# A Flamingo block with routed experts: one batch's logits back in its up products, one batch's attention weights by a DRAM trip, three expert loads moved

## Chip, cores and metric

The kernel runs on one core of a Trainium2 chip. The metric is the device time of one execution in microseconds; the kernel before has a median of 514.62 us over 11 runs (514.3 to 515.65). Another kernel's time is read against this.

## The reference, cut to what matters

There are four batches of 512 tokens, 512 wide, and a context of 512 rows, 256 wide, for each batch. All is float32.

```
x = x + tanh(g_xattn) * xattn(layernorm(x), ctx)
x = x + tanh(g_ffn)   * ffn(layernorm(x))

xattn: q = ctx @ Wq.T + bq;  k = ctx @ Wk.T + bk         (128 wide)
       attention = softmax(q @ k.T)                       (512 x 512 for each batch)
       out[l, m] = sum_n logits[l, n] * attention[m, n]   (logits = layernorm(x))

ffn:   shared = (silu(h @ Wg_s) * (h @ Wu_s)) @ Wd_s      (hidden 352)
       probs = sigmoid(h @ Wr + br + rb)                  (8 experts)
       the two highest of the 8, their probabilities over their sum as weights w
       routed = sum over the two of w * (silu(h @ Wg[e]) * (h @ Wu[e])) @ Wd[e]
```

The second sum over n needs the attention weights with n on the partitions: the softmax comes out with m on the partitions and has to be transposed. The same holds for the normalised rows h ahead of the feed-forward part.

## The kernel before, in words

**Memory.** One large tile, `wbig`, holds the eight experts' weights (`EW` columns each), and until they come in the parts behind the first `early = 3` experts are scratch for the attention: context, keys and queries, two transposed weight tiles `attT_v`, two transposed row tiles `xT_v`, the softmax tiles `ex_v`, the normalised tiles `xn_v` and their transposes `xnT_v`. Experts 0 to 2 overlay nothing. `ps_mm` gives four PSUM buffers, taken in turn by projections, energies, gate, up and all small products; `ps_out` two for outputs.

**Order.** Each engine runs its instructions in the fixed order of the built program; a scheduler makes that order from the program's dependencies, and `after(later, earlier)` adds dependencies by hand. SP (SyncE) issues most loads, ACT (ScalarE) those of the hidden tiles, POOL (GpSimd) the stores of tiles to DRAM and all indirect transfers. Each queue is in order too, and an instruction that waits holds up what is behind it. A DMA also waits for the eighth one before it of the same kind, whose semaphore it shares.

**Attention, batch by batch** (loop at lines 623 to 644). `attention_weights(i)` (line 339) projects keys and queries (L344, copied out by ScalarE, L351), makes four energy tiles (L362), and for each the row maximum (L364), the exponential (L367), and the division by the sum (L369, L370). For the first `AT_ONCE = 2` batches TensorE transposes the tiles at once, 128x128 at a time (`transposed`, L300, copied out by VectorE at L303). For later batches POOL stores each tile to DRAM in four column quarters (`to_quarters`, L321), SP loads it back (`from_quarters`, L327) with the rows regrouped, and VectorE turns it in 32x32 blocks (`turn`, L331; `attention_weights_turned`, line 389). This leaves the rows of the transposed tile in another order, which the host's `chunks` gives to the other operand, xT. `attention_out(i - 1)` (line 393) then makes batch i-1's output (L398, four tiles, each of four products that read all four transposed tiles), adds it to x (L402), takes the statistics (L310, L313), the inverse deviation (a power on POOL, L317), normalises (L411), and sends the normalised tiles on the same DRAM trip to `xz_d`. The last batch's normalised tiles are kept and transposed by TensorE (`last_turned`, line 647).

**Shared expert, hidden part.** `shared_hidden` (line 460) makes for each of the four chunks of 128 tokens of a batch four gate products (352 wide) and four up products (L471), SiLU on ScalarE (L479), the product on VectorE (L482), and a store to `hs_d` from ACT's queue. The router's weights stand behind the up weights. Where a batch is not in `alone`, the up products are 360 wide and give the logits (L481); where it is, they are 352 wide, and `logits` (line 443) makes the logits of several chunks by products of their own, 8 wide (L450), which can come ahead of the up products. `amid` lists what is put between the products of a chunk.

**Routing.** `route(b)` (line 498) takes the exponential, the two highest probabilities, and a running count by expert (`pre`, `cum`), each batch on top of the last. `places` (line 523) makes from it by two small products (L527) each token's place in a list, and `scatter_places` (line 557) writes tokens and weights to the list `slot_d` by eight indirect DMAs for each batch (L559). When all are there, POOL loads the list into `tab` (L711); VectorE spreads it (L720), small products (L653) pick each block's part, and from that come the indices by which POOL gathers rows for the routed blocks.

**The rest.** Line 656 on is the part between the attention and the list: batch 2's hidden chunks, batch 3's chunks, counting and expert loads, laid out by hand. Then come 16 tiles of the shared down product (`shared_down`, L575 and L602), with the list's small products behind the fifth and sixth, and 37 routed blocks (L796, L575).

Of the kernel before, what the change touches and what calls it, by code (L numbers as in the profile page):

```python
# [22 lines left out]
def flamingo_block(  # L23
# [17 lines left out]
    B, S, D = x.shape  # L41
# [7 lines left out]
    NS, ND, NCC, NN = S // P, D // P, C // P, N // P  # L49
# [49 lines left out]
    early = 3  # L99
# [104 lines left out]
    def load_expert(e, behind=None, parts=(True, True)):  # L204
        at = e * EW
        for src, f, part in ((wgu, 2 * H, parts[0]), (wd, D, parts[1])):
            n = src.shape[1] // P * f
            if part:
                load = nc.sync.dma_start(
                    out=wbig[:, at : at + n].rearrange("p (c f) -> p c f", f=f),  # L210
                    in_=src[e].rearrange("(c p) f -> p c f", p=P),
                )
                if behind is not None:
                    after(load, behind, "that goes first")
            at += n
# [17 lines left out]
    ones = fconst([P, P], "ones")  # L233
# [99 lines left out]
        )  # L333

    product = {}
    AT_ONCE = 2
    gain = {}

    def attention_weights(b):
# [49 lines left out]
    def attention_weights_turned(b, m, behind):  # L389
        t = turn(ex_v[m].rearrange("p (b w) -> p b w", b=NQ), attT_v[b % 2][:, :, ts(m, P)])  # L390
        after(t, behind, "they come in meanwhile")
# [45 lines left out]
        return turns  # L437

    lg_b = {}
    alone = {B - 2, B - 1}  # L440
    scatters = []

    def logits(b, lo=0, hi=NS):

        if lo == 0:
            lg_b[b] = small.tile([P, NS, E], F32, tag="lg", name=f"lg_{b}")
        pr = ps_mm.tile([P, hi - lo, E], F32, tag="mm", name="pr")
        for s in range(lo, hi):
            for c in range(ND):
                p = nc.tensor.matmul(  # L450
                    pr[:, s - lo, :], lhsT=xnT_v[b % 2][:, c, ts(s, P)], rhs=ws[:, c, 2 * H :],
                    start=(c == 0), stop=(c == ND - 1),
                )
                after(p, product["last"], "not too many small ones at once")
        nc.vector.tensor_tensor(
            lg_b[b][:, lo:hi, :], pr,
            bias_r.rearrange("p (o e) -> p o e", o=1).broadcast_to([P, hi - lo, E]), ALU.add,
        )

    def shared_hidden(b, lo=0, hi=NS, amid={}):  # L460

        route_too = b not in alone
        if route_too and lo == 0:
            lg_b[b] = small.tile([P, NS, E], F32, tag="lg", name=f"lg_{b}")
        wide = HR if route_too else H
        for s in range(lo, hi):
            pg = ps_mm.tile([P, H], F32, tag="mm", name="pg")
            pu = ps_mm.tile([P, wide], F32, tag="mm", name="pu")
            for c in range(ND):
                for dst, at, n in ((pg, 0, H), (pu, H, wide)):  # L470
                    product["last"] = nc.tensor.matmul(  # L471
                        dst, lhsT=xnT_v[b % 2][:, c, ts(s, P)], rhs=ws[:, c, at : at + n],
                        start=(c == 0), stop=(c == ND - 1),
                    )
                if c in amid:
                    amid[c]()
            filled = h_sb[(b * NS + s) % OUT]
            h = filled[:, :H]
            nc.scalar.activation(h, pg, AF.Silu)  # L479
            if route_too:  # L480
                nc.vector.tensor_add(lg_b[b][:, s, :], pu[:, H:], bias_r)  # L481
            done = nc.vector.tensor_mul(h, h, pu[:, :H])  # L482
            at = (b * NS + s) * NQ * P
            to_quarters(filled, hs_d[at : at + NQ * P, :], nc.scalar)
        return done
# [37 lines left out]
    def places(b, at, m1, m2, sel, pre):  # L523

        pl = ps_mm.tile([P, NS * E], F32, tag="mm", name="pl")
        for i, (l, r) in enumerate(((tri, sel), (ones, pre))):
            p = nc.tensor.matmul(  # L527
                pl, lhsT=l, rhs=r.rearrange("p s e -> p (s e)"),
                start=(i == 0), stop=(i == 1),
            )  # L530
            after(p, product["last"], "the routing takes its time")
        place = small.tile([P, NS, E], F32, tag="place", name=f"place_{b}")
        nc.vector.tensor_add(place, pl.rearrange("p (s e) -> p s e", e=E), first)  # L533
        tot = small.tile([P, NS, 1], F32, tag="tot", name=f"tot_{b}")
        nc.vector.tensor_add(tot, m1, m2)
        nc.vector.reciprocal(tot, tot)
        nc.vector.tensor_scalar_mul(tot, tot, tgf)
        todo = []
        for k, m in enumerate((m1, m2)):
            nc.vector.tensor_mul(at[k], at[k], place)  # L540
            pos = small.tile([P, NS, 1], F32, tag=f"pos{k}", name=f"pos{k}_{b}")
            nc.vector.tensor_reduce(pos, at[k], AX.X, ALU.add)
            posi = small.tile([P, NS], I32, tag=f"posi{k}", name=f"posi{k}_{b}")
            nc.vector.tensor_copy(posi, pos.rearrange("p s o -> p (s o)"))
            low = small.tile([P, NS], I32, tag=f"low{k}", name=f"low{k}_{b}")
            nc.vector.tensor_single_scalar(low, posi, P - 1, op=ALU.bitwise_and)
            ent = small.tile([P, NS, 2], F32, tag=f"ent{k}", name=f"ent{k}_{b}")
            nc.vector.tensor_tensor(
                ent[:, :, 0], token[:, b * NS : (b + 1) * NS], low, ALU.subtract
            )  # L550
            nc.vector.tensor_mul(
                ent[:, :, 1], m.rearrange("p s o -> p (s o)"), tot.rearrange("p s o -> p (s o)")
            )
            todo += [(ent[:, s, :], posi[:, s : s + 1]) for s in range(NS)]
        return todo

    def scatter_places(todo, behind=None):
        for what, where in todo:
            sc = nc.gpsimd.indirect_dma_start(  # L559
                out=slot_d, in_=what,  # L560
                out_offset=bass.IndirectOffsetOnAxis(ap=where, axis=0),
                in_offset=None,
            )
            tc.declare_no_dep(sc.ins, group="places", reason="no two tokens share a place")
            tc.add_to_no_dep_group("places", sc.ins)
            after(sc, cleared)
            if behind is not None:
                after(sc, behind, "it delays less there")
            scatters.append(sc)
# [48 lines left out]
    routed = None  # L618
# [4 lines left out]
    for i in range(B):  # L623
        attention_weights(i)
        if i + 2 < B:
            load_context(i + 2)
            load_rows(i + 2)
        if i < early:
            load_expert(i)
        if i > 0:  # L630
            power, done = attention_out(i - 1, halves(i - 2))
            if i + 1 < B:
                load_transposed(i + 1)
            if routed:
                scatter_places(places(i - 3, *routed), power)
        if i >= 2:
            for m in range(NS):
                attention_weights_turned(i, m, done)
                done = shared_hidden(i - 2, m, m + 1)
                if i == B - 1 and m == 0:  # L640
                    load_expert(early, done)
                if i == B - 1 and m == 1:
                    load_expert(early + 1, done, (True, False))
            routed = route(i - 2)
# [6 lines left out]
    def amid(dst, lhsT, rhs):  # L651

        p = nc.tensor.matmul(dst, lhsT=lhsT, rhs=rhs, start=True, stop=True)  # L653
        after(p, product["last"], "not too many small ones at once")

    routed = {}
    load_expert(4, None, (False, True))
    load_expert(5, None, (True, False))
    shared_hidden(B - 2, 0, 1, {1: lambda: logits(B - 2, 0, 2), 3: lambda: logits(B - 2, 2)})
    routed[B - 2] = route(B - 2)  # L660
    step = shared_hidden(
        B - 2, 1, 2, {1: lambda: last_turned(0, 2), 2: lambda: last_turned(2, NS)}
    )
# [1 line left out]
    shared_hidden(  # L665
        B - 2, 2, 3, {
            1: lambda: logits(B - 1, 0, 2), 2: lambda: logits(B - 1, 2),
            3: lambda: scatter_places(places(B - 2, *routed[B - 2])),
        }
    )  # L670
    routed[B - 1] = route(B - 1)
    step = shared_hidden(B - 2, 3)
    load_expert(6, step)
    step = shared_hidden(
        B - 1, 0, 1, {2: lambda: scatter_places(places(B - 1, *routed[B - 1]))}
    )
    back_early(step)

# [1 line left out]
    cum_b = fconst([P, E, JB], "cum_b")  # L680
# [2 lines left out]
    )  # L683
    pn = ps_mm.tile([P, 1], F32, tag="mm", name="pn")
    shared_hidden(
        B - 1, 1, 2, {1: lambda: amid(pn, cum_b.rearrange("p e j -> p (e j)"), ones[:, 0:1])}
    )
    used = fconst([P, 1], "used")
    nc.vector.tensor_tensor(used, pn, thr, ALU.is_gt)
# [26 lines left out]
    done = shared_out(0, 0, NS, (step, done))  # L716
# [240 lines left out]
```

## Time and profile before

| | |
|---|---|
| median of 11 runs | 514.62 us |
| the profiled execution | 514.6 us |
| its span | 512.6 us |
| granted TensorE clock, mean | 0.992 |
| TensorE's longest wait | 1.2 us, at the start |
| batch 1's output product begins, ends | 42.80, 60.15 us |
| batch 2's hidden chunks | 133.59 to 161.95 us |
| batch 3's hidden chunks | 161.95 to about 182.3 us |
| shared down product | 183.03 to about 222.3 us, two tiles later |
| first routed block begins | 223.30 us |
| last matmul ends | about 501.5 us |

The profile names engines PE (TensorE matmul), PEld (its weight loads), DVE (VectorE), ACT, POOL and SP. A float32 product is two records on PE. In a timeline a row is: start, length, engine, line, operation, written tile and read tiles, number of records, and in brackets the idle time before it and what ended that. The slices of the page cut the span into 40 parts; a digit is a busy share in tenths.

### The profile page before, as it was taken

The numbers are of one execution on the slowest core, as the hardware profiler recorded it, in microseconds if no ns is written. First come the engines' busy times: TensorE is split into PE (matmuls) and PEld (weight loads), VectorE is DVE, ScalarE is ACT, GpSimd is POOL, SyncE is SP. The second block draws the span as 40 slices with busy tenths as digits, with TensorE's granted clock in tenths as the row PEclk, the third lists the DMA queues.
The fourth block names the chain that finished last, engine by engine and source line by source line (L and its number), as shares of the span: only waits on it lengthen the run. The fifth ranks groups of instructions, "written<-read, shape, count | busy, mean of one in ns | idle before, by whom it ended". The sixth has DMA issues, their size and how long they took to land. (4 is left out here: it accounts for less than half of the span.)

```text
span 512.6 us, 5473 instructions
## 1 busy us (share of the span) xinstructions
PE 494.8 (97%) x1523; PEld 276.7 (54%) x1523; DVE 230.6 (45%) x542; ACT 93.8 (18%) x167; POOL 264.8 (52%) x293
## 2 busy tenths in 40 slices
PE   8999999999999999999999999999999999999981
PEld 4444464465677645445555555555555555555540
DVE  1898965855855256554223322332332233323210
ACT  3354034111241100000111111111111111111110
POOL 3005220271264702345777777777477777777231
PEclk9999999999999999999999999999999999999996
DMA  6999993579936999624566656665545666556333
GB/s 216 395 371 354 345 352 122 155 176 169 358 101 88 223 205 313 216 83 132 120 139 119 124 123 139 119 125 122 110 118 128 138 123 128 128 132 131 53 41 42
DMA packets 66589, 86.82 MB, mean 169 GB/s; under 512 B 32928, under 2 KB 39968, under 8 KB 66560
## 3 DMA queue, kind: packets, MB, share of 16 engines
q1 hardware_dynamic: 42480, 54.03, 34.8%
q0 software_dynamic: 13184, 25.88, 25.8%
q10 hardware_dynamic: 10896, 6.56, 5.1%
q8 instruction: 15, 0.25, 0.2%
q14 instruction: 14, 0.11, 0.1%
HBM read 55.73 MB, written 30.70 MB: 169 GB/s over the span
## 5 line engine op out<-in xcount | busy, mean ns | idle before, releaser
L761 POOL DMA_INDIRECT x_all<-xz_d,idx x148 | 141.3, 955 | 81.7 <-issue 34.4
L331 DVE STREAM_TRANSPOSE x_all<-x_all 128x512 f32<-128x512 f32 (+1 forms) x71 | 70.0, 986 | 157.1 <-DMA x_all<-by 135.5
L796 PE MATMUL rg<-wbig,x_all 128*128 x296 | 111.9, 460 | 1.7 <-issue 0.9
L796 PE MATMUL ru<-wbig,x_all 128*128 x296 | 111.7, 459 | 0.0
L575 PE MATMUL po<-wbig,x_all 128*128 x222 | 101.4, 592 | 0.7 <-DVE x_all L847 0.7
L796 PEld LDWEIGHTS rg<-wbig,x_all 128*128 128x128 f32 x296 | 55.9, 190 | 43.1 <-issue 18.4
L824 POOL DMA_INDIRECT out_x<-ws,idx x37 | 59.6, 1611 | 31.1 <-ACT ws L823 13.6
L796 PEld LDWEIGHTS ru<-wbig,x_all 128*128 128x128 f32 x296 | 56.2, 190 | 31.3
L575 PEld LDWEIGHTS po<-wbig,x_all 128*128 128x128 f32 x222 | 42.1, 190 | 44.0 <-issue 36.4
L398 PE MATMUL po<-wbig 128*128 128x512 f32 x128 | 56.4, 592 | 0.0
L471 PE MATMUL pg<-ws,wbig 128*128 128x352 f32 x128 | 49.3, 467 | 0.0
L471 PE MATMUL pu<-ws,wbig 128*128 128x360 f32 (+1 forms) x128 | 48.7, 462 | 0.0
L804 ACT ACTIVATE h_all<-rg 128x352 f32<-128x352 f32 x37 | 17.1, 463 | 171.6 <-PE rg L796 171.6
L317 POOL TENSOR_TENSOR rstd<-ve,mhalf 128x4 f32<-128x4 f32 x8 | 8.2, 1022 | 71.3 <-DVE ve L315 37.9
L823 ACT ACTIVATE ws<-po,wts 128x512 f32<-128x512 f32 x37 | 25.4, 687 | 104.2 <-PE po L575 101.2
L575 PE MATMUL po<-wsd,wqk 128*128 128x512 f32 x96 | 42.3, 595 | 0.5 <-DVE eoff_i L706 0.5
L398 PEld LDWEIGHTS po<-wbig 128*128 128x128 f32 x128 | 24.2, 190 | 29.4 <-issue 27.7
L559 POOL DMA_INDIRECT slot_d<-ent,posi x32 | 31.0, 968 | 17.3 <-issue 8.6
L471 PEld LDWEIGHTS pu<-ws,wbig 128*128 128x128 f32 x128 | 24.3, 190 | 13.6 <-DVE place L533 0.2
L575 PEld LDWEIGHTS po<-wsd,wqk 128*128 128x128 f32 x96 | 18.0, 190 | 22.1 <-issue 20.2
L471 PEld LDWEIGHTS pg<-ws,wbig 128*128 128x128 f32 x128 | 23.3, 190 | 11.6 <-issue 0.5
L806 DVE TENSOR_TENSOR x_all<-h_all,ru 128x352 f32<-128x352 f32 x34 | 17.6, 516 | 13.6 <-PE ru L796 7.4
(136 smaller groups left out, 339.2 us busy)
## 6 DMA issues: line engine op xcount, KB each, us to landing
wbig<-in_Wgu SPq DMA_DIRECT2D x8, 1408.0 KB, 12.0
by<-x_all SPq DMA_DIRECT2D x34, 192.0 KB, 3.2
x_all<-by SPq DMA_DIRECT2D x34, 192.0 KB, 2.4
wbig<-in_Wd SPq DMA_DIRECT2D x8, 768.0 KB, 11.0
x_all<-in_x SPq DMA_DIRECT2D x4, 1024.0 KB, 10.5
wbig<-in_xT SPq DMA_DIRECT2D x4, 1024.0 KB, 9.2
xz_d<-wbig POOLq DMA_DIRECT2D x16, 256.0 KB, 4.6
out_x<-x_all SPq DMA_DIRECT2D x16, 256.0 KB, 3.0
```

What stands on the lines that cost most here:

```text
L317: power = nc.gpsimd.tensor_tensor(rstd, ve, mhalf, ALU.pow)
L331: return nc.vector.transpose(dst.rearrange("p c (j b) -> p b c j", b=NQ), z.rearrange("p b (c i) -> p b c i", i=Q))
L398: product["last"] = nc.tensor.matmul(po, lhsT=xT_v[b % 2][:, c, ts(s, P)], rhs=attT_v[b % 2][:, c, :], start=(c == 0), stop=(c == NN - 1),)
L471: product["last"] = nc.tensor.matmul(dst, lhsT=xnT_v[b % 2][:, c, ts(s, P)], rhs=ws[:, c, at : at + n], start=(c == 0), stop=(c == ND - 1),)
L559: sc = nc.gpsimd.indirect_dma_start(out=slot_d, in_=what, out_offset=bass.IndirectOffsetOnAxis(ap=where, axis=0), in_offset=None,)
L575: product["last"] = nc.tensor.matmul(po, lhsT=hT[:, j, :], rhs=wdj(j), start=(j == 0), stop=(j == NF - 1))
L761: g = nc.gpsimd.indirect_dma_start(out=z[:, q, :], out_offset=None, in_=xz_d, in_offset=at(idx4[:, q, i : i + 1]),)
L796: nc.tensor.matmul(dst, lhsT=xgT[:, c, :], rhs=wbig[:, bass.ds(base[i] + (c * 2 * H + lo), H)], start=(c == 0), stop=(c == ND - 1),)
L804: silu = nc.scalar.activation(sg, pg, AF.Silu)
L806: nc.vector.tensor_mul(h[:, :H], sg, pu)
L823: nc.scalar.activation(y, po, AF.Copy, scale=wts[:, i : i + 1])
L824: nc.gpsimd.indirect_dma_start(out=out, in_=y, out_offset=at(idx[:, i : i + 1]), in_offset=None, compute_op=ALU.add)
```

## The change

Three edits, with what they bring along.

- `AT_ONCE` goes from 2 to 1: batch 1's softmax tiles make the DRAM trip and are turned by VectorE, behind `done`, the last normalised tile of batch 0; the host reorders xT for batches 1 to 3 rather than 2 and 3.
- Batch 2 leaves `alone`: its logits come from 360-wide up products. Its routing and batch 3's both come after batch 2's last chunk; their scatters move into batch 3's first and second chunk, and the counting product from behind the second to behind the third step of that chunk.
- Experts 0, 1 and 2 are loaded in the third turn of the loop, each behind a hidden chunk of batch 0, rather than one in each of the first three turns.

```
-    AT_ONCE = 2
+    AT_ONCE = 1
...
-    alone = {B - 2, B - 1}
+    alone = {B - 1}
...
-        if i < early:
-            load_expert(i)
...
+        if i == 1:
+            for m in range(NN):
+                attention_weights_turned(i, m, done)
         if i >= 2:
             for m in range(NS):
                 attention_weights_turned(i, m, done)
                 done = shared_hidden(i - 2, m, m + 1)
+                if i == 2 and m < early:
+                    load_expert(m, done)
...
-    shared_hidden(B - 2, 0, 1, {1: lambda: logits(B - 2, 0, 2), 3: lambda: logits(B - 2, 2)})
-    routed[B - 2] = route(B - 2)
+    shared_hidden(B - 2, 0, 1)
...
     shared_hidden(
         B - 2, 2, 3, {
             1: lambda: logits(B - 1, 0, 2), 2: lambda: logits(B - 1, 2),
-            3: lambda: scatter_places(places(B - 2, *routed[B - 2])),
         }
     )
-    routed[B - 1] = route(B - 1)
     step = shared_hidden(B - 2, 3)
+    routed = {b: route(b) for b in (B - 2, B - 1)}
     load_expert(6, step)
     step = shared_hidden(
-        B - 1, 0, 1, {2: lambda: scatter_places(places(B - 1, *routed[B - 1]))}
+        B - 1, 0, 1, {2: lambda: scatter_places(places(B - 2, *routed[B - 2]))}
     )
...
     shared_hidden(
-        B - 1, 1, 2, {1: lambda: amid(pn, cum_b.rearrange("p e j -> p (e j)"), ones[:, 0:1])}
+        B - 1, 1, 2, {
+            0: lambda: scatter_places(places(B - 1, *routed[B - 1])),
+            2: lambda: amid(pn, cum_b.rearrange("p e j -> p (e j)"), ones[:, 0:1]),
+        }
     )
...
-        "xT": np.concatenate([xT[:2], chunks(xT[2:])]),
+        "xT": np.concatenate([xT[:1], chunks(xT[1:])]),
```

## The prediction

> **What bounds the kernel now.** I read the engine shares and slices of the page first, then TensorE's waits, then each engine's timeline around the three edits, then the single transfers of the routing list.
>
> ```profile
> PE 494.8 (97%) x1523; PEld 276.7 (54%) x1523; DVE 230.6 (45%) x542; ACT 93.8 (18%) x167; POOL 264.8 (52%) x293
> ...
> PE   8999999999999999999999999999999999999981
> ...
> DMA  6999993579936999624566656665545666556333
> ```
>
> TensorE is busy in every slice up to the tail. Each of its waits is 1.2 us or less, so every matmul removed is time gained, and every new wait on TensorE is time lost in full. It runs its instructions in the order of the built program, so the question at each edit is when TensorE arrives at an instruction and when the data does.
>
> The span is 512.6 us, the profiled execution 514.6 us (2.0 around the span), the median of the runs 514.62. I add changes to 514.6. About 0.2% (1 us) is what a measurement of this kernel can tell from no change.
>
> **Part A: second batch's weights by the DRAM trip.** TensorE's timeline (start, length, line, tile):
>
> ```profile
> 22.83 3.60 PE L398 MATMUL po<-wbig 128*128 128x512 f32 x8
> 26.41 0.63 PE L300 MATMUL pt<-ident,wbig 128*128 128x128 f32 x4
> ...
> 34.21 7.03 PE L398 MATMUL po<-wbig 128*128 128x512 f32 x16
> 41.08 1.88 PE L344 MATMUL pp<-wbig,wqk 128*128 128x512 f32 x4
> ...
> 60.15 0.76 PE L471 MATMUL pg<-ws,wbig 128*128 128x352 f32 x2
> ```
>
> One 512-wide product is two records: 34.21 to 41.08 is eight products, 0.859 each. From 22.83 to 60.15 there are 40 of them (16 for batch 0's output, 4 projections and 4 energies of batch 2, 16 for batch 1's output), 34.4 us. The other 2.95 us are batch 1's 16 PE transposes and a 0.43 us wait among them. They go.
>
> What comes in: four stores by POOL, four loads by SP, four VectorE turns. In the built order the turns stand behind all four normalised tiles of batch 0 (the dependency on `done`) and one BN_STATS on batch 3's rows. VectorE's rows of before give the rates:
>
> ```profile
> 41.28 0.75 DVE L402 SCALAR_TENSOR_TENSOR x_all<-po,gain,x_all 128x512 f32<-128x512 f32 x1 [0.67 <-PE po L398]
> ...
> 44.30 2.00 DVE L411 TENSOR_SCALAR wbig<-x_all,mv,rstd 128x512 f32<-128x512 f32 x4 [1.12 <-POOL rstd L317]
> ...
> 55.60 2.02 DVE L331 STREAM_TRANSPOSE wbig<-wbig 128x512 f32<-128x512 f32 x2
> ```
>
> Without the transposes, batch 0's last output product ends near 37.65 (22.83, 16 products and one projection, 0.2 us for a PSUM buffer). Its sum on VectorE starts behind earlier work at 38.55; with its statistics it is at 39.9. The built order then has batch 2's gain ahead of batch 0's variance, so two POOL powers of 1.0 us run one after the other: 42.7. Normalising takes 1.95 (44.65), the BN_STATS 0.6, the four turns 0.95 each: 49.1. All four must be there, since each product reads all four tiles. TensorE would be free at 45.4 (the energies wait until 41.9 for ScalarE, whose key/query copy stands behind an activation that needs batch 2's offset). So batch 1's output runs from 49.2 to 62.95 instead of ending at 60.15: **+2.8 us**. If the two powers overlapped as before (4.7 us from the end of the product to the end of the normalising), it would be +0.5. Behind this wait on TensorE stand all of batch 1's output and the hidden chunks after it; VectorE's sums wait for them. The trip itself is off this path: the last store is issued near 31.4, and batch 2's and 3's stores and loads of the same kind landed in 2.7 to 8.3 us, so I expect its end at 38, at worst near 48, which would cost under 1 us. Batch 3's rows, queued on SP behind the trip's loads, are expected near 43, before the 44.65 at which they are wanted; late by 1 us costs 1 us.
>
> **Part B: third batch's logits in the up products.** Two groups of eight 8-wide products go:
>
> ```profile
> 136.03 1.85 PE L450 MATMUL pr<-ws,wbig 128*128 128x8 f32 x16
> 137.74 0.84 PE L471 MATMUL pg<-ws,wbig 128*128 128x352 f32 x2
> ```
>
> A group costs 1.71 plus 0.07 for the weight load behind it, 1.78. The 16 up products become 360 wide; 16 gate/up pairs took 19.15 us wide (60.15 to 79.30), 18.98 narrow. Net **-3.4**. The last batch's 16 transposes now come 3.5 us sooner after the start of this stage, and their copies stand behind a ScalarE table load and SiLU: about **+0.4**, from nothing to 0.8.
>
> **Part C: the routing of batches 2 and 3 moves behind batch 2's last chunk.** Let T be the end of that chunk on TensorE: 161.95 before; after, 161.95 + 2.8 - 3.4 + 0.4 - 0.44 (a pair of small products moves behind T) = 161.3. For batch 0, with the same scheme, T was 79.30 and the first routing instruction behind the exponential came at 82.12, T+2.8. The two routings now alternate on VectorE; the built order has 30 instructions from there to batch 2's selection, at 0.11 each (0.26 for the reciprocals): T+6.4. TensorE reaches the product with it after one chunk, T+4.75: **a new wait of 1.8** (1.2 to 2.3). Batch 3's other gate/up products stand behind it, and SiLU and VectorE's products wait for those. Then come a gate/up pair and the second product, T+8.2; place to first scatter took 1.6 (157.33 to 158.95): the scatters start at T+10.2, 171.5. Before, they started at T-3.0:
>
> ```profile
> 158.95 0.96 POOL L559 DMA_INDIRECT slot_d<-ent,posi  x1 [7.26 <-DVE ent L548]
> ...
> 178.48 0.96 POOL L559 DMA_INDIRECT slot_d<-ent,posi  x1 [0.30 <-DMA slot_d<-ent,posi]
> 190.26 0.59 POOL L711 DMA_DIRECT2D ws<-slot_d  x1 [10.82 <-DMA hs_d<-h_all]
> ```
>
> The 16 scatters took 19.5 us from first to last issue. The transfers issued at 178.48 and 190.26, with the time to landing last:
>
> ```profile
> slot_d<-ent,posi POOLq DMA_INDIRECT x1, 11.0
> ```
>
> ```profile
> ws<-slot_d POOLq DMA_DIRECT2D x1, 128.0 KB, 4.4
> ```
>
> The list's load left only when the last scatter had landed. TensorE needs the list at a fixed place, the small products behind five tiles of the shared down product:
>
> ```profile
> 183.03 13.14 PE L575 MATMUL po<-wsd,wqk 128*128 128x512 f32 x30 [0.53 <-DVE eoff_i L706]
> 196.01 0.98 PE L653 MATMUL pq<-pick,ws 128*128 128x39 f32 x8
> ```
>
> ```profile
> 195.01 0.74 DVE L720 COPY ws<-ws 128x128 f32<-128x128 f32 x4
> ```
>
> The copies that spread the list ended at 195.75: cover left before, 0.3 us. After: TensorE arrives at 196.0 + 2.8 - 3.4 + 0.4 + 1.8 = 197.6. Last scatter 171.5 + 19.4 = 190.9. Landing: 5.3 at best, 11.0 under the load of the last ones; expert 7's load and the hidden tiles' reads still run then, so nearer the second, 9.5, and 0.8 to the load: 201.2. The list's load 4.0 (4.4 before, 2.7 the least of such a size or double): 205.2. Spread and hand-over 1.3: 206.5. **+8.9**, with ends 3.3 (5.3 and 2.7) and 11. Behind the wait stand the rest of the shared products and the routed blocks; POOL's gathers wait for the same list. They start 5 us behind the small products and take 10; TensorE has 26 us of shared products behind them, so the first routed block does not wait again. Nothing later gives this time back: from 230 to 470 us TensorE is idle for 0.8 us of 240.
>
> The Trainium skill, "DMA: Bandwidth & Descriptors", section "Anatomy of one DMA — SWDGE (gpsimd) path", prices such a transfer at about 2.0 us plus its bytes at 436 GB/s. By it the last scatter would cost 2.0 and the list's load 2.3, the list would be ready at 197.3, and the wait would be gone: 516 in all. The 11.0 and 4.4 us above speak against using it here.
>
> **Part D: the clock.** No wait over 1.2 us stands inside the kernel, so what a long one does is seen only at its ends:
>
> ```profile
> 503.00:504.00 1.00, 0.00 (x0) 0.00 (x0) 0.00 (x0) 0.00 (x0) 0.78 (x1) 1.00 0.00 0
> ...
> 505.00:506.00 1.00, 0.00 (x0) 0.00 (x0) 0.00 (x0) 0.00 (x0) 0.00 (x0) 0.50 0.84 63
> ```
>
> ```profile
> 1.19 3.78 PE L150 MATMUL idle<-h_all 128*128 128x256 f32 x8 [1.19 <-DVE h_all L146]
> ```
>
> The column before the DMA share is the granted clock: it falls to 0.50 some 3.3 us after the last matmul (501.5). And the first eight 256-wide records take 0.45 each, against 0.43 for 512-wide ones later: half speed, for some 4 us. So a wait of 9 us should be followed by about 4 us at half speed: **+2.0** (0 to 2.3). Part A's gap of 3.8 us is on the edge; I count nothing, and keep 2.0 for the upper end.
>
> **Edits at no cost.** Experts 0 to 2 are first read at 223 us and, issued behind chunks near 70 to 82, land by 100 at 400 GB/s; were they late, block 0 would wait, but 120 us cover it. The loads that they stood in front of gain nothing, since TensorE did not wait for them. Batch 1's next reads of normalised rows stand around expert 0's load on SP; they are needed 20 us later. The host's reordering of one more batch of xT moves no work on the chip.
>
> **Sum.** 2.8 - 3.4 + 0.4 + 1.8 + 8.9 + 2.0 = +12.5: 514.6 + 12.5 = **527.1**.
>
> **Rivals.** (1) Short list: with the hidden tiles' reads held back while TensorE stands, scatters land in 5.3 to 7 and the list in 2.7; the wait is 3 to 5 and the clock may not fall: 518 to 522. For it: scatters landed in 5.9 to 7.8 at 160 to 163 us, when the DMA share was 0.20. Against: expert 7 is then loading. (2) Both gaps cost the clock and the landing is the old 11: 529 to 532. (3) Not slower: the list is in time. Place: the small products at 196; price: 10.9 us fall away; it decides if the list's copies are ready by 197.6, 8.9 us sooner than worked out, with Part A at its low end of 0.5: 513.9. Against it: POOL's pace alone puts the last scatter at 190.9, and two transfers follow. (4) The change does nothing to order: excluded by the built program, where the turns, the selection and the scatters stand as said.
>
> **Chances.** Forecast (523 to 529) 0.59; (1) 0.20; (2) 0.15; (3) 0.06, half of it within 0.2%, half faster. Range 518 to 531: it reaches into (1) and (2) and covers 3.3 to 11 for the list. Faster 0.03, same 0.03, slower 0.94.
>
> **What would show it.** Right: TensorE idle some 4 us before batch 1's output, released by VectorE's turns; idle 1.8 before the product with batch 2's selection; idle 7 to 11 before the small products at about 198, and a granted clock under 1 right behind. Scatters from about 171 to 191, their pace unchanged. No product of 8 columns for batch 2. Wrong if the scatters start earlier than T+8, if the last one lands within 6 us, or if TensorE's order has more shared products ahead of the list.

## The result, and the profile after

The changed kernel took **526.31 us** (median of 16 runs, 524.5 to 531.47); the kernel before, run beside it, 515.2 us (62 runs, 513.58 to 518.87). The ratio is 1.0215, with a 95% interval of 1.0198 to 1.0231: slower, by about 2% (11.1 us, where 12.5 was forecast). The first profiled execution took 530.42 us (span 528.6), near the top of its runs. The same kernel was profiled again in run e9: 527.07 us, span 525.3. Both profiles are used below.

The engine shares, slices and clock of the first profile:

```profile
PE 498.5 (94%) x1475; PEld 274.9 (52%) x1475; DVE 230.0 (44%) x544; ACT 91.2 (17%) x165; POOL 268.7 (51%) x297
...
PE   8995999999999893999999999999999999999992
...
PEclk9998899999999998799999999999999999999998
DMA  6989659949976668452465566665645666665532
```

TensorE has 48 records fewer (32 of the logits, 16 transposes), and two dents where it had none: in the fourth slice (near 45 us) and in the sixteenth (near 205 us). At both the clock is down as well. TensorE's chain of waits names them (total, times, longest):

```profile
PE pq L656 <- DVE ws L724: 8.7, 1, 8.7
PE po L398 <- DVE wbig L331: 3.5, 1, 3.5
PE pe L362 <- ACT wbig L351: 2.8, 2, 2.3
PE pl L527 <- DVE at L495: 1.6, 1, 1.6
```

They are the list, the turns of the second batch's weights, ScalarE's key/query copy ahead of the third batch's energies, and the third batch's selection. The first dent, in TensorE's timeline:

```profile
37.93 2.74 PE L344 MATMUL pp<-wbig,wqk 128*128 128x512 f32 x6
...
42.98 5.40 PE L362 MATMUL pe<-wbig 128*128 128x512 f32 x8 [2.32 <-ACT wbig L351]
51.91 14.43 PE L398 MATMUL po<-wbig 128*128 128x512 f32 x26 [3.53 <-DVE wbig L331]
```

and in VectorE's:

```profile
42.60 1.99 DVE L411 TENSOR_SCALAR wbig<-x_all,mv,rstd 128x512 f32<-128x512 f32 x4 [0.99 <-POOL rstd L317]
47.49 0.69 DVE L310 BATCH_NORM_STATS2 st<-x_all 128x6 f32<-128x512 f32 x1 [2.90 <-DMA x_all<-in_x]
48.10 3.76 DVE L331 STREAM_TRANSPOSE wbig<-wbig 128x512 f32<-128x512 f32 x4
```

The normalising ends at 44.6, as worked out. Then VectorE stands 2.90 us for the fourth batch's rows, with the turns behind it. The third batch's energies took 5.40 us for 3.70 before, most of them at half speed. The second dent, in the timelines of TensorE, POOL and VectorE:

```profile
173.70 0.38 PE L527 MATMUL pl<-sel,tri 128*128 128x32 f32 x2 [1.60 <-DVE at L495]
...
189.88 13.04 PE L575 MATMUL po<-wsd,wqk 128*128 128x512 f32 x30
211.65 1.93 PE L656 MATMUL pq<-pick,ws 128*128 128x39 f32 x8 [8.73 <-DVE ws L724]
```

```profile
177.14 0.96 POOL L559 DMA_INDIRECT slot_d<-ent,posi  x1 [16.83 <-DVE ent L551]
...
196.10 0.96 POOL L559 DMA_INDIRECT slot_d<-ent,posi  x1 [0.31 <-issue]
204.13 0.59 POOL L715 DMA_DIRECT2D ws<-slot_d  x1 [7.07 <-DMA h_all<-hs_d]
```

```profile
211.32 0.82 DVE L724 COPY ws<-ws 128x128 f32<-128x128 f32 x4 [7.06 <-DMA ws<-slot_d]
```

The scatters' train lasts 19.0 us from first to last issue, as before (19.5), 18 us later. The last scatter took 7.4 us to land, the list's load leaves 8.0 us behind its issue and takes 7.1 to land; TensorE stands in front of it. In the wait and behind it, the clock column (ahead of the DMA share) in stretches of 2 us:

```profile
208.00:210.00 2.00, 0.00 (x0) 0.00 (x0) 0.00 (x0) 0.00 (x0) 0.00 (x0) 0.54 1.06 407
...
214.00:216.00 2.00, 2.00 (x3) 0.67 (x2) 1.84 (x7) 0.00 (x0) 0.00 (x0) 0.50 0.53 178
```

Half speed lasts from 208.2 to 218.4. The whole difference can be laid out by landmarks of TensorE, each stretch in us:

| stretch | before | predicted | first profile | second profile (e9) |
|---|---|---|---|---|
| start to the third batch's hidden chunks (133.59 before) | 133.59 | +2.8 | +8.6 | +5.0 |
| those chunks (to 161.95) | 28.36 | -3.4 | -3.4 | -2.9 |
| to the shared down product (183.03) | 21.08 | +2.2 | +1.6 | +1.6 |
| to the list's products (196.01) | 12.98 | +8.9 | +8.8 | +9.5 |
| to the down product behind them (199.86) | 3.85 | +2.0 | +3.4 | +2.2 |
| to the first routed block (223.30) | 23.44 | 0 | 0 | 0 |
| to the end of the span | 289.3 | 0 | -3.0 | -2.7 |
| sum | 512.6 | +12.5 | +16.0 | +12.7 |

The pair of small products that moves behind the third batch's last chunk (0.44 us) is taken off in the second row and added in the third. There +1.6 came for +2.2 because a wait of 0.5 us ahead of the shared down product, which the kernel before has, is gone.

### The profile page after: what moved, and what is told of

Same layout as the page of the kernel before. It is cut to its first block, busy times and chain, and to the rows that moved or that the text cites. A ratio compares the mean times of both kernels' runs of the same rounds, so it can differ in the third digit from the quotient of the medians.

```text
span 528.6 us, 5399 instructions
## 1 busy us (share of the span) xinstructions
PE 498.5 (94%) x1475; PEld 274.9 (52%) x1475; DVE 230.0 (44%) x544; ACT 91.2 (17%) x165; POOL 268.7 (51%) x297
## 5 line engine op out<-in xcount | busy, mean ns | idle before, releaser
L398 PE MATMUL po<-wbig 128*128 128x512 f32 x128 | 59.1, 619 | 3.6 <-DVE wbig L331 3.5
L471 PE MATMUL pg<-ws,wbig 128*128 128x352 f32 x128 | 49.2, 466 | 0.0
L575 PE MATMUL po<-wsd,wqk 128*128 128x512 f32 x96 | 44.7, 622 | 0.0
L321 POOL DMA_DIRECT2D bya<-wbig x12 | 9.6, 798 | 37.7 <-DVE pre L520 20.2
## 6 DMA issues: line engine op xcount, KB each, us to landing
wbig<-in_Wd SPq DMA_DIRECT2D x8, 768.0 KB, 10.3
```

The costliest lines, as they stand in the source:

```text
L321: engine.dma_start(out=by.rearrange("(a p) w -> p a w", p=P), in_=src.rearrange("p (a w) -> p a w", a=NQ))
L398: product["last"] = nc.tensor.matmul(po, lhsT=xT_v[b % 2][:, c, ts(s, P)], rhs=attT_v[b % 2][:, c, :], start=(c == 0), stop=(c == NN - 1),)
L471: product["last"] = nc.tensor.matmul(dst, lhsT=xnT_v[b % 2][:, c, ts(s, P)], rhs=ws[:, c, at : at + n], start=(c == 0), stop=(c == ND - 1),)
L575: product["last"] = nc.tensor.matmul(po, lhsT=hT[:, j, :], rhs=wdj(j), start=(j == 0), stop=(j == NF - 1))
```

## The experiments

The twelve runs were made on three chips: e1 to e4 on one, e5 to e8 on a second, e9 to e12 on a third. Each ratio is to the kernel before on the same chip, which took 522.19, 521.67 and 518.78 us there, spread over 7 to 12 us. Why it is above 515 there is what e5 and e11 are about. Effects are therefore read from waits and landmarks first.

**e1: without the trip.** The second batch's weights are turned by TensorE again.

```
-    AT_ONCE = 1
+    AT_ONCE = 2
...
-        if i == 1:
-            for m in range(NN):
-                attention_weights_turned(i, m, done)
...
```

> The changed kernel with the second batch's weights transposed by TensorE again (edit A undone; the later routing and the later expert loads stay). Theory: the list's wait of some 9 us and the slow clock behind it stay, since they come from the later routing; what goes is TensorE's wait for the turns and the clock it costs. 522 to 525 us. Rival 1 (the trip is the whole loss): 511 to 513. Rival 2 (the trip is hidden and costs nothing): 526 to 527. On the trace: no wait of po on a stream transpose near 50 us, a wait of pq of 7 to 11 us near 200.

Measured: 527.06 us, ratio 1.0136 (1.0058 to 1.0215). No wait for turns is left, and the selection still waits 1.6. The list:

```profile
PE pq L653 <- DVE ws L721: 10.8, 1, 10.8
PE pl L527 <- DVE at L495: 1.6, 1, 1.6
```

The time is not the theory's 522 to 525 but the second rival's, and that of the changed kernel on the third chip (e9, 527.49), though the fourth batch's energies start at 85.03 instead of 89.42. Against e9's profile, the first routed block begins only 1.65 us sooner (237.01 for 238.66): the list wait is 1.4 longer and half speed lasts 13.65 us instead of 10.24. The end is 3.6 longer (290.2 from the first block to the span's end, for 286.6). So between these two profiles the trip's cost is real at its place, and is given back at two others.

**e2: without the logits' move.** The third batch's logits, routing and scatters stand as before; trip and experts as in the changed kernel.

```
-    alone = {B - 1}
+    alone = {B - 2, B - 1}
...
-    shared_hidden(B - 2, 0, 1)
+    shared_hidden(B - 2, 0, 1, {1: lambda: logits(B - 2, 0, 2), 3: lambda: logits(B - 2, 2)})
+    routed[B - 2] = route(B - 2)
...
+            3: lambda: scatter_places(places(B - 2, *routed[B - 2])),
...
```

> The changed kernel with the third batch's logits and the whole routing order as before (edit B undone; trip and later expert loads stay). Theory: no wait for the list and none for the selection; left is the trip's price, 1 to 5 us over before: 516 to 520 us. Rival 1 (the trip is the whole loss): 526. Rival 2 (trip free, loss all routing): 512 to 515. On the trace: pq waits under 1 us, po waits 3 to 7 us for the turns.

Measured: 526.13 us, ratio 1.0115 (1.0032 to 1.0198). The list wait is gone. That fits the late dispatch as its cause, but does not show it: the list had landed at 200.8, and TensorE came for it only at 212.97, some 11 us late by other waits and the clock behind them. (e10 shows it.) The longest of these I had not thought of:

```profile
PE pw L656 <- ACT h_all L479: 5.7, 1, 5.7
...
PE pb L656 <- ACT h_all L479: 2.0, 1, 2.0
```

TensorE waits for SiLU to free its gate tile, in the last two hidden chunks. ACT is late because of a store of hidden units (who waited, for what):

```profile
ACT h_all L479 <- DMA hs_d<-wbig: 10.6, 1, 10.6
```

And ahead of that store VectorE had stood for a scatter; e5 takes this step apart.

```profile
DVE ent L551 <- DMA slot_d<-ent,posi: 4.2, 1, 4.2
```

**e3: the list's products four tiles later.**

```
     done = shared_out(0, 0, NS, (step, done))
+    done = shared_out(1, 0, 4)
...
-    shared_out(1, 0, 1)
+    done = shared_out(2, 0, 1)
...
-    shared_out(1, 1, 2)
+    done = shared_out(2, 1, 2)
...
-    shared_out(1, 2)
-    shared_out(B - 2)
+    done = shared_out(2, 2, 4)
```

> The changed kernel with the list's spread and small products put four tiles of the shared down product (10.3 us) later. Theory: the wait of 8.7 us and the slow clock behind it are both gone, some 12 us, and the gathers still end before the first routed block: 513 to 517 us. Rival (the wait only moves, to the first routed blocks, whose rows are gathered 10 us later): 520 to 526, with TensorE idle near 225 to 240 us. On the trace: clock 1.00 from 190 to 240.

Measured: 521.3 us, ratio 1.0019 (0.9977 to 1.0061). No wait for the list is left, but not all of it is won:

```profile
PE po L575 <- DVE wqk L331: 3.6, 1, 3.6
```

TensorE now waits for a hidden tile on its way back from DRAM, whose read landed late beside the last scatters and expert 7's load, and half speed for 3.4 us followed. Of some 12 us (9.5 and 2.2 behind it) 6.6 are gained against e4 beside it (527.91), which has the list at its place.

**e4: experts 0 to 2 loaded early again.**

```
+        if i < early:
+            load_expert(i)
...
-                if i == 2 and m < early:
-                    load_expert(m, done)
```

> The changed kernel with experts 0 to 2 loaded one in each of the first three turns again (third edit undone). Theory: the later loads cost nothing by themselves; undone, their bytes fall into the trip's stretch, stores, loads and the fourth batch's rows land later, and TensorE waits longer before the second batch's output: 527 to 532 us. Rival (the moved loads are what slows the middle of the kernel): 515 to 522. On the trace: the wait for the turns grows from 3.5 us.

Measured: 527.91 us, ratio 1.0152 (1.0069 to 1.0235).

```profile
PE pq L656 <- DVE ws L724: 10.0, 1, 10.0
PE pe L362 <- ACT wbig L351: 3.8, 2, 3.4
...
PE po L398 <- DVE wbig L331: 0.7, 1, 0.7
```

The list wait, and the first routed block at 239.80, lie by those of the changed kernel's two profiles (242.32, 238.66), so the place of these loads is worth nothing that can be told. The theory's longer wait for the turns did not come. It is short, 0.7 us, because the third batch's energies ran later (44.28) and at half speed; the fourth batch's start at 88.49, for 93.05 and 89.42.

**e5: the kernel before, profiled again.** No edit.

> The kernel before, unchanged, profiled a second time. In its first profile POOL issued the list's load at 190.26, it landed 4.4 us later, DVE copied the list from 195.01 and TensorE used it at 196.01: at most about 1 us was to spare. In the runs beside the first four experiments this kernel took 516.3 to 528.0 us, 514 to 519 elsewhere. Theory (the kernel before already stands at the edge of the list wait): where its time is above 515, the chain of TensorE's waits shows a wait for the list's copy of about the excess, at half price again for the clock behind it where the wait is over some 3 us; at 514 to 515 it shows none. Rival (the excess is elsewhere, in the block loop or at the ends): a time above 516 without a row of waiting for the list, and block 0 starting within 1 us of 223.3.

Measured: 525.4 us (span 523.4), beside runs of itself of 517.43 to 526.83. Both theories fell: the list is in time, and the excess is ahead of the routed blocks (233.41 for 223.30), not in them or at the end. TensorE's timeline, and ACT's:

```profile
188.39 0.29 PE L653 MATMUL pw<-pick,eoff 128*1 128x39 f32 x2 [5.35 <-ACT h_all L479]
```

```profile
187.87 0.46 ACT L479 ACTIVATE h_all<-pg 128x352 f32<-128x352 f32 x1 [10.31 <-DMA hs_d<-wbig]
```

It is e2's wait, in the kernel before, and it starts at VectorE. What the scatters write to the list stands in small tiles, two of a kind, taken in turn by the batches. So VectorE can write the fourth batch's entries only when the second batch's last scatter has landed. VectorE's timeline in the first profile, then in e5:

```profile
161.51 0.37 DVE L551 TENSOR_TENSOR ent<-m,tot 128x4 f32<-128x4 f32 x2
```

```profile
161.63 0.17 DVE L551 TENSOR_TENSOR ent<-m,tot 128x4 f32<-128x4 f32 x1
166.40 0.17 DVE L551 TENSOR_TENSOR ent<-m,tot 128x4 f32<-128x4 f32 x1 [4.60 <-DMA slot_d<-ent,posi]
```

That scatter left at 150.73 in the first profile and landed after 10.1 us, less than 1 us before its tile was wanted. In e5 it left at 150.84 and landed after 15.4. Behind VectorE's wait its hidden product began at 167.41 instead of 162.72, and the store of these hidden units left at 167.96 instead of 163.28. Beside the scatters it took 19.4 us instead of 14.0; ACT stood until it had landed, near 187.4, and 5.3 us of TensorE with 6.8 us at half speed followed. Why the second batch's scatter landed later in e5 no run tells.

**e6: the kernel before with the list's products four tiles later** (e3's edit).

> The kernel before with the list's twelve products four output tiles later (behind five tiles of the second batch's and later shared products instead of one), nothing else. Theory (the kernel before stands at the edge of the list wait): the load then has some 12 us to spare, no run of it waits for the list, and the runs draw together near 514 to 516, while the kernel before beside it spreads as far as 528: ratio about 0.985 to 0.995 where the kernel before is spread, 1.00 where it is at 514. Rival (the spread has another cause): the same median and the same spread as the kernel before, ratio 1.00. A price that could show: TensorE waiting 3.6 us for the turn of a hidden tile, as in the changed kernel with the list later.

Measured: 522.0 us (518.82 to 524.67), ratio 1.0006 (0.997 to 1.0042). The rival holds: the same median, the spread hardly less (5.9 us for 9.4), and the wait is that of e5, behind 3.0 us of VectorE for the same scatter:

```profile
PE pw L653 <- ACT h_all L479: 5.1, 1, 5.1
```

**e7: the fourth batch's rows first on SP.**

```
     for i in range(B):
+        if i == 1:
+            load_rows(i + 2)
         attention_weights(i)
         if i + 2 < B:
             load_context(i + 2)
-            load_rows(i + 2)
+            if i != 1:
+                load_rows(i + 2)
```

> The changed kernel with the load of the fourth batch's rows issued on SP ahead of the second batch's rows of weights back from DRAM, instead of behind them. Theory (the 3.5 us wait for the turns is half a late load of rows: DVE's statistics of the fourth batch waited 2.9 us for them, in order ahead of the turns): the wait of the 8-long attention products for the turns falls to 0 to 1.5 us, the statistics wait for nothing, and batch 0's hidden units start some 2 to 3 us sooner than 68.75; the list is not touched, so the wait before its products stays near 8.7 to 10 us and the time near 523 to 526. Rival (the trip itself is late: four stores landing 6.6 to 8.7 us after their issue): moving the load ahead puts the trip's reads later, the wait moves from the rows to the reads and stays at 3 to 4 us, and the time doesn't move.

Measured: 530.63 us, ratio 1.0185 (1.0134 to 1.0236): not better.

```profile
PE pq L659 <- DVE ws L727: 10.8, 1, 10.8
PE po L398 <- DVE rs L369: 4.7, 1, 4.7
...
PE pe L362 <- ACT wbig L351: 1.2, 2, 0.8
```

The wait for the rows went (0.21 us left) and the turns ended at 49.97, 1.3 to 1.9 sooner. But the energies came sooner too, so TensorE stood longer, and the clock fell for 6.8 us. The fourth batch's energies start at 90.23, no earlier than in e9 (89.42). Neither text foresaw this. From the late rows on (40.17) to the end of the turns VectorE stands for no more than 0.4 us, so here its own order (statistics, normalising, turns) holds the turns.

**e8: logits alone, dispatch and list later.** From the kernel before: the logits in the up products, early experts, no trip, both places in the fourth batch's second chunk, the list five tiles later.

```
-    alone = {B - 2, B - 1}
+    alone = {B - 1}
...
+            1: lambda: scatter_places(places(B - 2, *routed[B - 2])),
+            2: lambda: scatter_places(places(B - 1, *routed[B - 1])),
...
+    done = shared_out(1, 0, 4)
+    done = shared_out(2, 0, 1)
...
```

> The kernel before with the third batch's logits in its up products alone (no trip, experts loaded as before), its places and the fourth batch's put into the fourth batch's second hidden chunk at the second and third steps, so that neither waits for the router's arithmetic, and the list's products four to five output tiles later. Theory (the change holds one true gain, 3.4 us of logits off TensorE, which its order of selection and list gives back): no wait of the selection's products, no wait for the list, 514.6 - 3.4 = 511 us, ratio about 0.99 against the kernel before at 514.6 and less where that one is spread. Rival (the dispatch cannot be put off for nothing: hidden tiles' trips through DRAM run beside the scatters and come back late): a wait of 3 to 6 us for the turn of a hidden tile, as in the changed kernel with the list later, and a time of 514 to 517. A second rival: the list comes later than its later products, wait 2 to 8 us and the clock behind it, 514 to 523.

Measured: 520.3 us, ratio 0.9983 (0.9952 to 1.0014). The theory's 511 did not come. Neither selection nor list waits; the first rival's wait is there, a little longer than it said:

```profile
PE po L575 <- DVE wqk L331: 6.3, 1, 6.3
```

**e9: the changed kernel again.** No edit.

> The changed kernel, unchanged, on the same chip as the three runs that follow. Where the kernel before takes 517 to 527 us on this chip (its second profile showed TensorE waiting 5.3 us in the last hidden chunk for ACT, which itself waited 10.3 us for a hidden tile's store), the question is whether the changed kernel is lengthened too. Theory (the scatters crowd the queues; before pays in the hidden tiles' stores, after in the list): 525 to 530 us, a wait for the list of 8.5 to 11 us and no wait of the last hidden chunk, so the ratio shrinks from 1.0215 to 1.01 or so. Rival (this chip is slower for every kernel by the same amount): 533 us, ratio 1.02.

Measured: 527.49 us (527.07 to 528.39), ratio 1.0179 (1.0136 to 1.0223). No wait in the hidden chunks, and

```profile
PE pq L656 <- DVE ws L724: 9.4, 1, 9.4
PE po L398 <- DVE wbig L331: 3.5, 1, 3.5
PE pe L362 <- ACT wbig L351: 3.4, 2, 3.0
```

The theory holds: the changed kernel does not pay what the kernel before pays on these chips. It writes the fourth batch's entries later (near 177 in the first profile, where the second batch's last scatter had left at 159.35). The ratio's interval still overlaps that of the first runs.

**e10 and e11: eight scatters fewer.** In the changed kernel, and with the same replacement in the kernel before. Both leave out the third batch's scatters, so the list lacks a quarter of its entries:

```
-        B - 1, 0, 1, {2: lambda: scatter_places(places(B - 2, *routed[B - 2]))}
+        B - 1, 0, 1, {2: lambda: places(B - 2, *routed[B - 2])}
```

> The changed kernel without the third batch's eight scatters of places (the list then lacks a quarter of its entries; all arithmetic on VectorE stays). Theory (the list wait is made by the train of sixteen scatters behind one another and their landing): the train ends eight scatters, 10 us, sooner, near 186; the list's load leaves some 8 to 10 us sooner and TensorE's wait for the list of 8.7 to 10.8 us falls to 0 to 1.5 us, the half-speed stretch behind it goes too, and the time falls by 9 to 13 us, to 514 to 518. Rival (the list is late because of its load and the hidden tiles' transfers, whatever the train): the wait stays above 5 us and the time above 520.

> The kernel before without the third batch's eight scatters of places (the list lacks a quarter of its entries; all arithmetic on VectorE stays). Theory (on this chip the scatters hold up the stores of hidden units, which ACT and through it TensorE wait for): the 5.3 us wait in the last hidden chunk falls to 0 to 1 us, no half-speed stretch follows it, and the time is 512 to 516 with little spread, ratio 0.98 to 0.99. Rival (the excess comes of the loads of expert weights that share the queues with the hidden tiles): the wait stays at 3 to 6 us and the ratio within 0.5% of 1.

Measured for e10: 517.06 us, ratio 0.9967 (0.9937 to 0.9996), 10.4 us under e9 on the same chip. TensorE's timeline, and POOL's:

```profile
200.42 1.08 PE L656 MATMUL pq<-pick,ws 128*128 128x39 f32 x8 [0.40 <-DVE ws L724]
```

```profile
193.76 0.59 POOL L715 DMA_DIRECT2D ws<-slot_d  x1 [8.17 <-DMA slot_d<-ent,posi]
```

The load leaves 8.4 us sooner than in e9 (202.20) and the wait of 9.4 is 0.4. For e11: 514.08 us (513.89 to 514.69), ratio 0.9908 (0.9875 to 0.994). No wait of VectorE for a scatter, none in the hidden chunks, no half speed before the last matmul, and the spread is 0.8 us instead of 6.6. So the scatters cause both: the list wait of the changed kernel, and the wait of the hidden chunks in the kernel before.

**e12: logits and experts, without the trip, the list four tiles later** (e1's and e3's edits together).

> The changed kernel with the second batch's weights turned by TensorE as before and the list's products four tiles later: two of its four parts, logits and experts, with room for the list. Theory (the parts add): against the changed kernel with the list later (521.3, block 0 from 232.99) the trip's 5.2 us go (its start of the third batch's attention products 93.69 against 88.46 without the trip), 514 to 517, ratio about 0.99 on this chip; no list wait, a wait of the selection of 1.6 us, a wait for the turn of a hidden tile of 2 to 6 us. Rival (what the trip cost comes back as a longer wait for the hidden tiles, since the dispatch is not moved): ratio 1.00, the wait for the turn 6 us or more.

Measured: 517.98 us (514.96 to 520.22), ratio 0.9991 (0.996 to 1.0022).

```profile
PE po L575 <- DVE wqk L331: 1.8, 1, 1.8
PE pl L527 <- DVE at L495: 1.6, 1, 1.6
```

The profiled execution's span is 515.2 for e3's 520.0. The waits are those of the theory or less, but the ratio is the rival's: no difference from the kernel before. None of the versions that do all the work beat it.

## Why the prediction was right, and where not

**The list (+8.9): right, and shown.** It measured 8.8 and 9.5. Taking it away by place (e3) or by half the train (e10) removes the wait. Two of its terms were off and nearly cancelled, which is luck. From the last scatter to the list's load I had 10.3 us: 8.0 and 9.2 came. For the load I had 4.0: 7.1 and 6.5 came, beside expert 7's load. By an estimate from the Trainium skill ("DMA: Bandwidth & Descriptors", "Anatomy of one DMA — SWDGE (gpsimd) path": about 2.0 us and the bytes at 436 GB/s) that load would have cost 2.3 us; 7.1 and 6.5 decide against it here.

**The clock (+2.0): right in kind**, 3.4 and 2.2 in size. I counted none for part A; the first profile paid 3.0 us there, e9 nothing.

**The logits (-3.4 and +0.4): right**, -3.4 and -2.9 with the transposes, where these terms and the pair of small products made -3.4.

**The selection (+1.8): right**, 1.60 in each of the profiles that route both batches behind the last chunk and place them at once. The prediction's own times give 1.65 (T+6.4 less T+4.75); 1.8 is a little more than they carry.

**The trip (+2.8): mis-sized.** It measured 8.6 and 5.0; the fourth batch's energies start at 84.4 to 85.3 in the seven profiles without the trip and at 88.5 to 93.1 in the seven with it. The step that failed is the time of the turns. Batch 3's rows were "expected near 43, before the 44.65 at which they are wanted": in the first profile, issued at 39.67 behind the trip's reads, they landed 7.8 us later, near 47.4, and cost the turns 2.9 us. In e9 they cost 1.2, and the normalising ended 1.0 later than worked out. So batch 1's output began at 51.9 and 51.3, not 49.2. The rest of the 8.6 is the clock: half speed from 51.2 to 58.0 made that output 3.0 us longer. ScalarE's copy, too, let the energies start only at 42.98 and 44.05, not 41.9, but TensorE waited 3.5 us for the turns behind them all the same, so by itself this cost nothing.

**The end (0): missed.** The span ends 8.1 us behind the last matmul for 11.1 before. In the trace POOL's closing drain takes 5.3 to 5.7 us in the seven profiles with the trip and 8.6 to 9.1 in the seven without it. e1 and e12 differ from the changed kernel and e3 by the trip alone, so it is the trip that shortens it; why, no run tells. It pays for half of the trip, and so 527.1 stands closer to the measured 526.31 than its terms deserve: that is luck.

**What stayed out of sight** is that the kernel before was itself at an edge. I had noted 0.3 us of cover at the list. The nearer edge was the tile of entries and, behind it, the hidden tiles' stores: less than 1 us of cover in a profile that shows no wait. e5 and e11 showed it. The 1 us that I held to be what a measurement can tell was too small for the same reason: this kernel's own runs spread over 5 us beside the first result and over 7 to 12 on the three chips. What makes the scatters land later there stays open.

## What to carry to other kernels

In these runs a long train of small transfers was always paid by someone. Moved, it changed who waited (VectorE for a tile that a scatter still read, stores of hidden units, a list, a tile on its way back). So follow every transfer that will stand beside it at its new place, and every buffer that it holds. A wait taken off a queue is won only as far as the next data on the same path are ready: the list's products four tiles later gained 6.6 of some 12 us. One clean profile does not say how much cover there is: look for the transfer that landed just in time, and take a second profile.

## What the runs showed of the hardware

**The clock is decided on fixed stretches of 3.41 us, not by a gap's length.** Half speed lasted 3.41, 6.83, 10.24 or 13.65 us wherever it began and ended inside a profile: one to four times 3.41. The full speed between two falls fits the same grid: in the first profile 150.19 us (44 times) and 307.2 us (90 times). In the first profile the clock fell at 44.3 behind a gap of 2.3 us. In e9 it did not fall behind gaps of 3.0 and 3.5 us. The stretches of 1 us there, first profile then e9:

```profile
45.00:46.00 1.00, 1.00 (x2) 0.34 (x1) 0.00 (x0) 0.00 (x0) 1.00 (x3) 0.50 1.04 369
```

```profile
47.00:48.00 1.00, 0.75 (x2) 0.00 (x0) 1.00 (x2) 0.00 (x0) 0.67 (x1) 1.00 1.06 408
...
50.00:51.00 1.00, 0.00 (x0) 0.00 (x0) 1.00 (x2) 0.00 (x0) 0.00 (x0) 1.00 0.26 94
```

The stretch that ended with the first profile's fall had TensorE busy for 1.36 of its 3.41 us (40%). The two that e9's gap of 3.5 us falls into held 1.48 and 1.8 us (43 and 53%), those of its gap of 3.0 us 1.6 and 2.2. Over all fourteen profiles, up to the last matmul, every stretch at full speed with TensorE busy for 40% or less was followed by half speed, and none with 43% or more. An estimate from these: the limit lies between 40 and 43%. Back to full speed takes more: in e2 and e6 a stretch at half speed, busy for 65 and 52%, was followed by another. The Trainium skill, "TensorE: Matmul & The Clock Gate", "Part 1: The HAM clock gate", speaks of a free-running window of 4096 cycles, which agrees with the 3.41 us; it has the clock fall only after a window of idleness, and the 2.3 us gap speaks against that.

**The same 128 KB load of the list** landed in 2.7 (e2, e5), 4.4 (before), 5.6 (e10), 6.5 (e9) and 7.1 us (first profile after). The DMA engines moved some 120 and 150 GB/s beside the first two, 290 to 340 beside the others.
